# Second layer of a two-layer cross attention: value products for batches 0 to 3, 4 to 6 and 7, with a fixed order on VectorE and earlier finishing

## The chip, the core and the metric

The kernel runs on one core of a Trainium2 chip. The metric is the device time of one execution in microseconds. The core has five engines that work side by side and meet at semaphores: PE (TensorE, matrix products; PEld is its loading of weights), DVE (VectorE, elementwise work and reductions), ACT (ScalarE), POOL (GpSimd) and SP (here only a queue that issues DMAs). Each engine takes its own instructions in the order in which they stand.

## The reference

Eight batches of 100 queries (`x`, 1024 wide) attend to a context of 1444 rows of 512. There are two layers, one after the other, both on the same context:

```python
# layer 0
Q = x @ Wq + bq;  K = ctx @ Wk + bk;  V = ctx @ Wv + bv
x = x + (softmax(Q @ K.T / 32, axis=keys) @ V) @ Wo + bo
# layer 1: the softmax runs over the queries, not over the keys
q = x @ Wq + bq;  k = ctx @ Wk + bk;  v = ctx @ Wv + bv
w = softmax(q @ k.T / 32, axis=queries)
y = w @ v + x
out = (y - mean(y)) * rsqrt(var(y) + 1e-6) * gamma + beta
```

All numbers are float32.

## The kernel before

The kernel folds the weights first: it multiplies Wq by Wk and, in layer 0, Wv by Wo, so that the context enters the scores and the weighted sums directly. Queries are held transposed in one tile, `xT` (128 partitions, 8 blocks of the feature dimension, 800 columns: 100 for each batch). Layer results are added into it.

The second layer goes through the batches one after the other in `alternated(b, ...)`. A batch has 48 steps n. At each step PE does one matmul of `A` (`weighted_rows`: softmax weights times context rows, four blocks of 100 columns, in a bank of the pool `psum2`) and one piece of the scores of batch b+2 (`scores`: 44 pieces of about 131 columns, in four banks of the pool `psum`, which has six). After the last step ACT copies A to a tile `A1T` (L524). When the scores of a batch are complete, ACT copies them to `prob` with a scale and a bias (L554), DVE turns `prob` into rows of keys with 16 block transposes (`transposed`, L589), and DVE and ACT make the softmax of it (`softmax_rows`: maxima L656, exponentials L658, reciprocals L661, products L662). POOL adds up the weights over the keys (`weight_sums`, ending at L680). At step 8 of every odd batch PE transposes two batches' sums into a bank of `psum` (`weight_totals`, tile `wsum_ps`, L687), and DVE reduces this bank to `r` (L689).

The values are applied afterwards, to A of several batches together. `seven_products` makes a product of two halves by two halves with seven products of halves instead of eight; its names are X, Z, Y, W, and X is used three times, Y twice. `put` and `add` take the banks' contents away: for the second layer both are additions into `xT` on DVE (`add_to_queries`, L612). The right-hand sums T (`right_sums`) are made of A by DVE; the left-hand sums of Wv by POOL in `project1_sums`. Before the change:

- batches 0 to 4 go through `project1_halves` (seven products, each 8 matmuls of 250 columns) after batch 5; the sums partly overwrite A in place;
- batches 5 and 6 go through `project1` (32 plain matmuls of 200 columns, L718) after batch 6;
- batch 7 goes through `project_last` at the end (L784).

In batch 5 the scores of batch 7 run at two pieces a step (`doubled`), so that they are complete after 22 steps.

`finish` brings a batch to its output: eight transposes on PE into two banks of `psum` (`untransposed`, tile `z`, L741), DVE adds the bias times r (L745) and takes statistics (L751, L756), DVE, POOL and ACT normalise (rstd L758 and L759, z L760, L762, L763), and POOL issues the output's DMA (L764). Before the change batches 0, 1 and 2 are finished during batch 6, from steps 0, 14 and 28 on; 3 and 4 around and inside `project1`; 5 and 6 during batch 7. Batch 7 ends the program: its output leaves in two halves, one by the SP queue and one by the ACT queue (L766 to L768).

PE's order is written out by hand (`tc.manual_schedule(engines={PE})`); that of the other engines comes from a scheduler. The pools give a bank to the next user in the order of the program, and the new user waits for the last reader of the old contents.

Of the kernel before, what the change touches and what calls it, by code (L numbers as in the profile page):

```python
# [24 lines left out]
F32 = mybir.dt.float32  # L25
# [5 lines left out]
P = 128  # L31
# [13 lines left out]
PT = 4  # L45
G = 4
GT = G * T
G1 = 5
SCALE = 1.0 / math.sqrt(E)
EPS = 1e-6  # L50

# [2 lines left out]
def two_layer_cross_attention(ctx: ExitStack, tc: tile.TileContext, a: dict, out: bass.AP):  # L54
# [18 lines left out]
        return stream.tile([P, E + L], F32, tag="unit", name=name)  # L73

    def wide(name):
        t = work.tile([P, LC * G1 * T], F32, tag="AT", name=name, bufs=2)
        return t[:, : LC * GT].rearrange("p (c t) -> p c t", c=LC)

    def row(name):
        return work.tile([P, E], F32, tag="row", name=name, bufs=3)  # L80

    def weight_rows(name):
        return work.tile([P, MC * T + QD * (-(-T // QD)) - T], F32, tag="wT", name=name, bufs=3)


    ones = const.tile([P, P], F32, tag="ones", name="ones")
# [36 lines left out]
    def run(*parts):  # L123

        parts = list(parts)
        while parts:
            parts = [g for g in parts if next(g, parts) is not parts]
# [19 lines left out]
                    skip_group_check=True,  # L147
                )

    def combine(to, x, y, op, engine=nc.vector):  # L150
        for t, p, q in zip(to, x, y):
            engine.tensor_tensor(t, p, q, op)

# [1 line left out]

        return [t[:, i, :] for i in range(n)]

    def left_sums(A, S, some=(0, 1, 2, 3), engine=nc.vector):
        A11, A12, A21, A22 = A
        todo = ((S[0], A21, A22, ALU.add), (S[1], S[0], A11, ALU.subtract))  # L160
        todo += ((S[2], A11, A21, ALU.subtract), (S[3], A12, S[1], ALU.subtract))
        for n in some:
            combine(*todo[n], engine)
# [7 lines left out]

    def seven_products(name, A, Bs, S, T_, nb, width, put, add, left=None, right=None):

        left, right = left or (lambda n: None), right or (lambda n: None)
        A11, A12, A21, A22 = A
        B11, B21, B12, B22 = Bs

        def pair(n, bank=bank):
            return [bank(f"{name}_{n}{j}") for j in range(2)]

        def product(banks, lhs, rhs, fresh):
            half_product(banks, lhs, rhs, fresh, nb, width)
# [12 lines left out]
        add(0, 0, Z)  # L198
        Y = pair("y")
        product(Y, S[0], T_[0], True)  # L200
        put(1, 1, Y)
        yield
        right(3)
        product(X, S[1], T_[1], False)
        put(0, 1, X)
        yield
        left(2)
        right(2)
        W = pair("w", bank2)
        product(W, A22, T_[3], True)  # L210
        yield
        left(3)
        product(X, S[2], T_[2], False)
        add(1, 1, X)
        put(1, 0, X)
        add(1, 0, W)
        yield
        product(Y, S[3], B22, False)
        add(0, 1, Y)
        yield  # L220


    def weight_products(name, left, right, l_width, r_width, scaled):
# [32 lines left out]

        A11, A12, A21, A22 = lefts(0, 0), lefts(1, 0), lefts(0, 1), lefts(1, 1)
        B11, B12, B21, B22 = rights(0, 0), rights(0, 1), rights(1, 0), rights(1, 1)
        extra = [work.tile([P, LC * G1 * T], F32, tag="AT", name=f"{name}_s{n}", bufs=2) for n in range(2)]
        S1 = [extra[i // 2][:, i % 2 * 768 : i % 2 * 768 + lh] for i in range(H)]  # L260
        T1 = [extra[i // 2][:, i % 2 * 768 + lh : (i % 2 + 1) * 768] for i in range(H)]

# [267 lines left out]
    def scores(s, layer, cT, softmax, alone=False):  # L530
# [29 lines left out]
            )  # L560
        w = s["rows"] = weight_rows(f"w{layer}_{b}")
        s["w"] = w[:, : MC * T].rearrange("p (c t) -> p c t", t=T)
        softmax(s, parts)
        yield

    def softmax0(s, parts):

        b, p = s["b"], s["p"]
        maxima = small.tile([T, len(parts)], F32, tag="maxima", name=f"maxima_{b}")
        for n, part in enumerate(parts):  # L570
            nc.vector.tensor_reduce(maxima[:, n : n + 1], p[:, part], AX.X, ALU.max)  # L571
# [7 lines left out]
        transposed(s, 0 if b else PT)  # L579

    def transposed(s, m0):

        p, w = prob[s["b"] % len(prob)], s["rows"]
        for q in range(-(-T // QD) - 1, -1, -1):
            for r in range(P // QD):
                nc.vector.transpose(  # L589
                    blocks(w, r, m0 * T + q * QD, T, MC - m0),  # L590
                    blocks(p, q, m0 * MR + r * QD, MR, MC - m0),
                )

    def blocks(t, quad, first, step, n):

# [12 lines left out]
    def add_to_queries(blocks, t0, width, banks):  # L608
        n = len(blocks) // len(banks)
        for j, ps in enumerate(banks):  # L610
            to = xT[:, blocks[j * n] : blocks[j * n] + n, t0 : t0 + width]
            nc.vector.tensor_tensor(to, to, ps[:, : n * width].rearrange("p (n t) -> p n t", n=n), ALU.add)  # L612

    def value_sums(w):

# [26 lines left out]

    def softmax1(s, parts):

        transposed(s, 0)
        for m in range(0, MC, GM):
            softmax_rows(s, m)
        weight_sums(s)
# [48 lines left out]
        left_sums(A, S, engine=nc.gpsimd)  # L697
        return A, S

    def project1_halves(A, S, At):  # L700

        n = G1 * T // 2
        Bs = [[At[:, 2 * k + i, g * n : (g + 1) * n] for i in range(2)] for g in range(2) for k in range(2)]
        t1 = work.tile([P, LC, GT], F32, tag="gT", name="o1_t1", bufs=3).rearrange("p c t -> p (c t)")
        T_ = ([t1[:, i * n : (i + 1) * n] for i in range(2)], Bs[0], Bs[2], Bs[1])

        def add(r, g, banks):
            add_to_queries([4 * r + i for i in range(4)], g * n, n, banks)

        run(seven_products("o1", A, Bs, S, T_, 4, n, add, add, right=lambda k: right_sums(Bs, T_, (k,))))  # L710

    def project1(b0, n, A, between):

        t0, t1 = b0 * T, (b0 + n) * T
        for e in range(EC):
            ps = bank(f"o1_{b0}_{e}")
            for k in range(LC):
                nc.tensor.matmul(  # L718
                    ps[:, : n * T], wv1[:, k, e * P : (e + 1) * P], A[:, k, : n * T], start=(k == 0), stop=(k == LC - 1)
                )  # L720
            to = xT[:, e, t0:t1]
            nc.vector.tensor_tensor(to, to, ps[:, : n * T], ALU.add)
            if e == EC // 2 - 1:
                between()

    def untransposed(s):

# [25 lines left out]
    def normalise(s):  # L753
# [7 lines left out]
        if b < B - 1:  # L761
# [1 line left out]
            nc.gpsimd.tensor_tensor(z, z, beta[:T], ALU.add)  # L763
            nc.gpsimd.dma_start(out=out[b], in_=z)  # L764
            return
        for half, queue in ((slice(0, E // 2), nc.sync), (slice(E // 2, E), nc.scalar)):  # L766
            nc.vector.scalar_tensor_tensor(z[:, half], z[:, half], rstd, beta[:T, half], ALU.mult, ALU.add)
            queue.dma_start(out=out[b][:, half], in_=z[:, half])  # L768

# [32 lines left out]

        return scores(batches[b], layer, *loaded(load_features(b)), softmax, alone=True)

    def alternated(b, layer, softmax, dst, doubled=False):

        nxt = b + 2 < B  # L810
        c, *cT = loaded(load_rows(b), *([load_features(b + 2)] if nxt else []))
# [1 line left out]
        ahead = scores(batches[b + 2], layer, *cT, softmax) if nxt else iter(())  # L813
        for _ in range(MC * LC):
            next(A)
            for _ in range(2 if doubled else 1):
                next(ahead, None)
            yield

    key_bias = [c0, None]  # L820
# [36 lines left out]
    run(first_scores(0, 1, softmax1))  # L857
    run(steps)
    run(first_scores(1, 1, softmax1))
    A1 = {}  # L860

    finished = {(B - 2, 0): 0, (B - 2, 14): 1, (B - 2, 28): 2, (B - 1, 6): G1, (B - 1, 22): G1 + 1}
    finishing = []
    for b in range(B):
        if b in (0, G1, B - 1):
            n = {0: G1, G1: 2, B - 1: 1}[b]
            t = work.tile([P, LC * G1 * T], F32, tag="AT", name=f"A1T_{b}", bufs=2)
            t = t[:, : LC * n * T].rearrange("p (c t) -> p c t", c=LC)
            for i in range(n):
                A1[b + i] = (t, t[:, :, i * T : (i + 1) * T])  # L870
        for n, _ in enumerate(alternated(b, 1, softmax1, A1[b][1], b + 3 == B)):
            if b % 2 and n == 8:
                weight_totals(batches[b - 1 : b + 1])
            if (b, n) in finished:
                finishing.append(finish(batches[finished[b, n]]))
            finishing = [f for f in finishing if next(f, finishing) is not finishing]
        if b == B - 1:
            run(untransposed(batches[b]))
        if b == 1:
            AS = project1_sums(wv1)  # L880
        if b == G1:
            project1_halves(*AS, A1[0][0])
        if b == B - 2:
            run(finish(batches[G1 - 2]))
            project1(G1, 2, A1[G1][0], lambda: run(finish(batches[G1 - 1])))
        if b == B - 1:
            project_last(batches[b], A1[b][0])


# [22 lines left out]
```

## Time and profile before

| what | us |
|---|---|
| median of three runs | 642.72 (641.82 to 643.38) |
| the profiled execution's own time | 642.46 |
| its span, first to last instruction | 640.7 |
| PE busy in the span | 631.4 |
| DVE busy in the span | 450.0 |
| second layer, batch 3 (48 steps, A and scores) | 503.6 to 523.5 |
| batch 5, with doubled scores | 542.9 to 563.0 |
| seven products for batches 0 to 4 | 563.0 to 586.6 |
| batch 6, with three finishes | 586.6 to 600.3 |
| products for batches 5 and 6, with one finish inside | 600.5 to 612.2 |
| batch 7, with two finishes | 612.2 to 624.6 |
| last products, and the end of the span | 625.5 to 640.7 |

The mean granted clock of PE is 0.996 of full speed. A group in the profile is named by its line, engine and operation, with the tiles it writes and reads. In a timeline each row has the start, the busy time, the engine, the line and the operation; brackets at the end give the idle time of the engine ahead of it and who ended it. PE's float32 matmuls leave two records each, transposes one.

### The profile page before, as it was taken

How to read it: one execution, taken by the hardware profiler on the slowest of the kernel's cores; microseconds unless marked ns; L12 is line 12 of the kernel's file. 1: busy time of each engine (PE TensorE's matmuls, PEld its weight loads, DVE VectorE, ACT ScalarE, POOL GpSimd, SP SyncE). 2: the span in 40 equal slices, each digit the busy share in tenths (PEclk: the TensorE clock that was granted, in tenths of full speed). 3: DMA queues.
4: the chain of work that ended last, by engine and by line, in shares of the span. 5: the costliest groups of instructions: out<-in, count | busy, mean ns of one | idle time of the engine just before them, and what ended most of it. 6: DMA issues, size and time to landing. Idle time of an engine off the chain costs nothing.

```text
span 640.7 us, 9823 instructions
## 1 busy us (share of the span) xinstructions
PE 631.4 (99%) x3920; PEld 518.4 (81%) x3920; DVE 450.0 (70%) x848; ACT 132.2 (21%) x337; POOL 101.7 (16%) x121
## 2 busy tenths in 40 slices
PE   9999999999999999999999999999999999999994
PEld 8886445568885999999998655556999999999992
DVE  5999959669723775566655798238777655896994
ACT  1010010100203333212330000123433244330221
POOL 5000000009200000000010000007211222112773
PEclk9999999999999999999999999999999999999998
DMA  8928018000089788988996203055889998940122
GB/s 292 383 101 316 0 56 333 0 1 0 2 288 367 263 310 295 329 311 311 310 315 237 97 1 131 1 176 202 284 298 315 313 307 317 303 172 1 52 78 77
DMA packets 47961, 127.28 MB, mean 199 GB/s; under 512 B 3944, under 2 KB 6504, under 8 KB 47916
## 3 DMA queue, kind: packets, MB, share of 16 engines
q1 hardware_dynamic: 45454, 119.63, 53.8%
q0 software_dynamic: 2064, 6.56, 3.2%
q8 instruction: 31, 0.51, 0.3%
q10 hardware_dynamic: 398, 0.47, 0.2%
q14 instruction: 14, 0.11, 0.1%
HBM read 123.36 MB, written 3.28 MB: 198 GB/s over the span
## 4 chain that ended last, share of the span: by engine, by line
PE 84%; issue 5%; POOL 5%; DVE 4%; ACT 2%; POOLq 0%; DVEq 0%; ACTq 0%
PE s L542 23%; PE A L513 20%; PE qk_x L141 7%; PE g_x L141 5%; PE qk_y L141 4%; PE g_y L141 3%; PE vo_x L141 3%; DVE w L589 3%; PE o_x L141 3%; POOL z L763 2%; PE qk_w L141 2%; PE vo_y L141 2%; PE qk_z L141 2%; PE g_w L141 2%; PE g_z L141 2%
## 5 line engine op out<-in xcount | busy, mean ns | idle before, releaser
L513 PE MATMUL A<-w,c 120*128 120x100 f32 (+1 forms) x1536 | 245.9, 265 | 0.0
L513 PEld LDWEIGHTS A<-w,c 120*128 120x128 f32 (+1 forms) x1536 | 215.5, 190 | 0.8
L589 DVE STREAM_TRANSPOSE w<-prob 32x384 f32<-32x384 f32 (+1 forms) x256 | 143.7, 561 | 46.4 <-ACT prob L554 15.8
L542 PE MATMUL s<-cT,g0T 128*100 128x131 f32 (+2 forms) x592 | 122.7, 296 | 0.0
L542 PE MATMUL s<-cT,g1T 128*100 128x131 f32 (+2 forms) x592 | 119.3, 296 | 0.0
L542 PEld LDWEIGHTS s<-cT,g0T 128*100 128x100 f32 x592 | 78.3, 167 | 8.3
L542 PEld LDWEIGHTS s<-cT,g1T 128*100 128x100 f32 x592 | 77.5, 167 | 8.9 <-ACT g1T L418 0.9
L554 ACT ACTIVATE prob<-s,c 100x393 f32<-100x393 f32 (+2 forms) x64 | 35.1, 560 | 116.9 <-PE s L542 116.6
L658 ACT ACTIVATE w<-w,negmax 120x100 f32<-120x100 f32 (+1 forms) x96 | 34.8, 364 | 75.1 <-DVE negmax L656 75.1
L469 POOL TENSOR_SCALAR xT<-xT,L_xattn_bo 128x800 f32<-128x800 f32 x8 | 20.8, 2607 | 133.1 <-PE qk_x L141 133.1
L571 DVE TENSOR_REDUCE maxima<-prob 100x1 f32<-100x394 f32 (+3 forms) x32 | 16.6, 528 | 28.1 <-ACT prob L554 27.9
L141 PE MATMUL qk_x<-qk 128*128 128x256 f32 x128 | 29.8, 393 | 0.0
L141 PEld LDWEIGHTS qk_x<-qk 128*128 128x128 f32 x128 | 24.7, 197 | 4.1 <-ACT qk L278 0.4
L850 POOL DMA_DIRECT2D vectors<-in_L_xattn_gamma x1 | 0.6, 602 | 163.2 <-DMA c<-in_ctx 163.2
L675 POOL TENSOR_TENSOR part<-w 120x500 f32<-120x500 f32 x8 | 10.0, 1248 | 103.5 <-PE s L542 47.3
L302 DVE SCALAR_TENSOR_TENSOR qk_L_xattn_bk<-qk,L_xattn_bk,qk_L_xattn_bk 128x1024 f32<-128x1024 f32 x14 | 17.9, 1276 | 4.0 <-DMA qk<-in_L_xattn_WqT 3.9
L612 DVE TENSOR_TENSOR xT<-xT,o_x 128x400 f32<-128x400 f32 (+1 forms) x24 | 13.5, 600 | 7.9 <-PE o_x L141 7.8
L418 ACT ACTIVATE g1T<-g_x,k 128x400 f32<-128x400 f32 x6 | 3.6, 594 | 74.2 <-PE g_x L141 63.8
L658 ACT ACTIVATION_READ_ACCUMULATOR w<-w,negmax 120x1 f32 (+1 forms) x96 | 17.9, 187 | 0.0
L763 POOL TENSOR_TENSOR z<-z,vectors 100x1024 f32<-100x1024 f32 x7 | 16.5, 2356 | 8.3 <-ACT z L762 8.3
L762 ACT ACTIVATE z<-z,rstd 100x1024 f32<-100x1024 f32 x7 | 8.0, 1149 | 39.7 <-POOL rstd L759 39.6
L662 DVE TENSOR_TENSOR w<-w,rtotal 120x400 f32<-120x400 f32 (+1 forms) x24 | 15.2, 633 | 0.5
(216 smaller groups left out, 871.8 us busy)
## 6 DMA issues: line engine op xcount, KB each, us to landing
cT<-in_ctxT SPq DMA_DIRECT2D x64, 722.0 KB, 6.7
c<-in_ctx SPq DMA_DIRECT2D x48, 768.0 KB, 7.5
c<-in_ctx SPq DMA_DIRECT2D x16, 512.0 KB, 6.6
vo<-in_L_xattn_Wo SPq DMA_DIRECT2D x8, 512.0 KB, 7.2
qk<-in_L_xattn_WqT SPq DMA_DIRECT2D x8, 512.0 KB
qk<-in_L_xattn_WqT SPq DMA_DIRECT2D x15, 256.0 KB, 5.4
qk<-in_L_xattn_WkT SPq DMA_DIRECT2D x15, 256.0 KB, 6.2
c<-in_ctx SPq DMA_DIRECT2D x16, 224.0 KB, 6.4
```

The costliest lines, as they stand in the source:

```text
L141: nc.tensor.matmul(banks[n // per][:, n % per * width : (n % per + 1) * width], lhs[i][:, n * P : (n + 1) * P], rhs[i], start=(fresh and i ...
L302: nc.vector.scalar_tensor_tensor(acc, src, cols[v][:, h : h + 1], acc, ALU.mult, ALU.add)
L469: nc.gpsimd.tensor_scalar(xT[:, e, :], xT[:, e, :], out_bias[:, e : e + 1], None, ALU.add)
L513: nc.tensor.matmul(ps[:, k * T : (k + 1) * T], c[m // CQ][:r, m % CQ, k * P : (k + 1) * P], w[:r, m, :], start=(m == 0 and k == 0), stop=( ...
L542: nc.tensor.matmul(banks[n // per][:T, cuts[n] - o : cuts[n + 1] - o], q[:, k, t0 : t0 + T], cT[k][:, cuts[n] : cuts[n + 1]], start=(k == ...
L554: nc.scalar.activation(p[:, part], ps[:T, : part.stop - part.start], AF.Identity, bias=key_bias[layer][:T, b : b + 1], scale=SCALE,)
L571: nc.vector.tensor_reduce(maxima[:, n : n + 1], p[:, part], AX.X, ALU.max)
L589: nc.vector.transpose(blocks(w, r, m0 * T + q * QD, T, MC - m0), blocks(p, q, m0 * MR + r * QD, MR, MC - m0),)
L612: nc.vector.tensor_tensor(to, to, ps[:, : n * width].rearrange("p (n t) -> p n t", n=n), ALU.add)
L658: nc.scalar.activation(w[:r, m0 + m, :], w[:r, m0 + m, :], AF.Exp, bias=negmax[:r, m : m + 1], accum_out=total[:r, m : m + 1])
L662: nc.vector.tensor_tensor(w[:r, grp, :], w[:r, grp, :], rtotal[:r].unsqueeze(2).to_broadcast([r, GM, T]), ALU.mult)
L763: nc.gpsimd.tensor_tensor(z, z, beta[:T], ALU.add)
```

## The change

It touches the second layer only.

- The value products are made in three sets: batches 0 to 3, batches 4 to 6, and batch 7. The first two go through a new `project1`, both with seven products: 8 matmuls of 200 columns each for the first, of 150 for the second. The first set runs right after batch 3, the second right after batch 6. The sums T have a tile of their own and are all made at the start.
- Within `project1` DVE's instructions are kept in program order (the wrapper `Vector`). In the first set the 16 block transposes of batch 5's softmax are dealt out between the additions: 3 each after Z, Y, the second X and W, and the rest at the end. For this `softmax` has become a generator (`s["softmax"]`), and `transposed` yields after each transpose.
- W's additions come right behind W where `put` is `add`.
- The doubled scores in batch 5 are gone: one piece a step everywhere.
- Finishes begin at other steps: batches 0, 1 and 2 in batch 4 (steps 2, 16, 30), batch 3 in batch 5 (step 4), batches 4, 5 and 6 in batch 7 (steps 2, 15, 28).
- The last output's first half leaves by the ACT queue, its second by SP.
- The AT tiles are 400 columns by 4 instead of 500 by 4.

```diff
-G1 = 5
+SETS = (range(0, 4), range(4, 7), range(7, 8))
...
+        if put is add:
+            add(1, 0, W)
         yield
         left(3)
         product(X, S[2], T_[2], False)
         add(1, 1, X)
         put(1, 0, X)
-        add(1, 0, W)
+        if put is not add:
+            add(1, 0, W)
...
-        softmax(s, parts)
+        s["softmax"] = softmax(s, parts)
+        if (layer, b) != (1, SETS[0][-1] + 2):
+            run(s["softmax"])
...
-                nc.vector.transpose(
+                vector.transpose(
                     blocks(w, r, m0 * T + q * QD, T, MC - m0),
                     blocks(p, q, m0 * MR + r * QD, MR, MC - m0),
                 )
+                yield
...
+    def project1(bs, A, S, At, between):
+
+        n, t0 = len(bs) * T // 2, bs[0] * T
         Bs = [[At[:, 2 * k + i, g * n : (g + 1) * n] for i in range(2)] for g in range(2) for k in range(2)]
...
+        sums = work.tile([P, LC, GT], F32, tag="gT", name=f"o1_{t0}_t", bufs=3).rearrange("p c t -> p (c t)")
+        T_ = [[sums[:, (2 * k + i) * n : (2 * k + i + 1) * n] for i in range(2)] for k in range(4)]
...
+        vector.in_order = True
+        right_sums(Bs, T_)
+
+        room = iter((0, 3, 3, 3, 3))
+        for _ in seven_products(f"o1_{t0}", A, Bs, S, T_, 4, n, add, add):
+            for _ in range(next(room, 0)):
+                next(between, None)
+        run(between)
+        vector.in_order = False
...
-        for half, queue in ((slice(0, E // 2), nc.sync), (slice(E // 2, E), nc.scalar)):
+        for half, queue in ((slice(0, E // 2), nc.scalar), (slice(E // 2, E), nc.sync)):
...
-            for _ in range(2 if doubled else 1):
-                next(ahead, None)
+            next(ahead, None)
...
-    finished = {(B - 2, 0): 0, (B - 2, 14): 1, (B - 2, 28): 2, (B - 1, 6): G1, (B - 1, 22): G1 + 1}
+    finished = {(4, 2): 0, (4, 16): 1, (4, 30): 2, (5, 4): 3, (7, 2): 4, (7, 15): 5, (7, 28): 6}
...
+    for bs in SETS:
+        t = wide(f"A1T_{bs[0]}").rearrange("p c t -> p (c t)")[:, : LC * len(bs) * T]
+        t = t.rearrange("p (c t) -> p c t", c=LC)
+        for i, b in enumerate(bs):
+            for n, _ in enumerate(alternated(b, 1, softmax1, t[:, :, i * T : (i + 1) * T])):
+                if b % 2 and n == 8:
+                    weight_totals(batches[b - 1 : b + 1])
+                if (b, n) in finished:
+                    finishing.append(finish(batches[finished[b, n]]))
+                finishing = [f for f in finishing if next(f, finishing) is not finishing]
+            if b == 1:
+                AS = project1_sums(wv1)
+        if b < B - 1:
+            project1(bs, *AS, t, batches[bs[-1] + 2]["softmax"] if bs[0] == 0 else iter(()))
+    run(untransposed(batches[B - 1]))
+    project_last(batches[B - 1], t)
```

More of the change, by code (lines that the diff above doesn't have):

```diff
@@ L75, in wide @@
     def wide(name):
-        t = work.tile([P, LC * G1 * T], F32, tag="AT", name=name, bufs=2)
-        return t[:, : LC * GT].rearrange("p (c t) -> p c t", c=LC)
+        return work.tile([P, LC, GT], F32, tag="AT", name=name, bufs=2)
     def row(name):
@@ L83, in weight_rows, with __getattr__, call @@
         return work.tile([P, MC * T + QD * (-(-T // QD)) - T], F32, tag="wT", name=name, bufs=3)
+    class Vector:
+        in_order = False
+        def __getattr__(self, op):
+            def call(*args):
+                ins = getattr(nc.vector, op)(*args)
+                return tc.keep_in_program_order(ins) if self.in_order else ins
+            return call
+    vector = Vector()
     ones = const.tile([P, P], F32, tag="ones", name="ones")
@@ L148, in half_product, with combine @@
                 )
-    def combine(to, x, y, op, engine=nc.vector):
+    def combine(to, x, y, op, engine=vector):
         for t, p, q in zip(to, x, y):
@@ L156, in chunks, with left_sums @@
         return [t[:, i, :] for i in range(n)]
-    def left_sums(A, S, some=(0, 1, 2, 3), engine=nc.vector):
+    def left_sums(A, S, some=(0, 1, 2, 3), engine=vector):
         A11, A12, A21, A22 = A
@@ L258, in weight_products @@
         B11, B12, B21, B22 = rights(0, 0), rights(0, 1), rights(1, 0), rights(1, 1)
-        extra = [work.tile([P, LC * G1 * T], F32, tag="AT", name=f"{name}_s{n}", bufs=2) for n in range(2)]
+        extra = [wide(f"{name}_s{n}").rearrange("p c t -> p (c t)") for n in range(2)]
         S1 = [extra[i // 2][:, i % 2 * 768 : i % 2 * 768 + lh] for i in range(H)]
@@ L578, in softmax0 @@
         nc.scalar.activation(p, p, AF.Copy, scale=rtotal)
-        transposed(s, 0 if b else PT)
+        yield from transposed(s, 0 if b else PT)
     def transposed(s, m0):
@@ L611, in add_to_queries @@
             to = xT[:, blocks[j * n] : blocks[j * n] + n, t0 : t0 + width]
-            nc.vector.tensor_tensor(to, to, ps[:, : n * width].rearrange("p (n t) -> p n t", n=n), ALU.add)
+            vector.tensor_tensor(to, to, ps[:, : n * width].rearrange("p (n t) -> p n t", n=n), ALU.add)
     def value_sums(w):
@@ L643, in softmax1 @@
     def softmax1(s, parts):
-        transposed(s, 0)
+        yield from transposed(s, 0)
         for m in range(0, MC, GM):
@@ L698, in project1_sums @@
         return A, S
-    def project1_halves(A, S, At):
-        n = G1 * T // 2
+    def project1(bs, A, S, At, between):
+        n, t0 = len(bs) * T // 2, bs[0] * T
         Bs = [[At[:, 2 * k + i, g * n : (g + 1) * n] for i in range(2)] for g in range(2) for k in range(2)]
-        t1 = work.tile([P, LC, GT], F32, tag="gT", name="o1_t1", bufs=3).rearrange("p c t -> p (c t)")
-        T_ = ([t1[:, i * n : (i + 1) * n] for i in range(2)], Bs[0], Bs[2], Bs[1])
+        sums = work.tile([P, LC, GT], F32, tag="gT", name=f"o1_{t0}_t", bufs=3).rearrange("p c t -> p (c t)")
+        T_ = [[sums[:, (2 * k + i) * n : (2 * k + i + 1) * n] for i in range(2)] for k in range(4)]
         def add(r, g, banks):
[L708 to L724, printed above, removed]
+            add_to_queries([4 * r + i for i in range(4)], t0 + g * n, n, banks)
+        vector.in_order = True
[6 more added lines that the diff above has]
+        vector.in_order = False
     def untransposed(s):
@@ L803, in first_scores, with alternated @@
         return scores(batches[b], layer, *loaded(load_features(b)), softmax, alone=True)
-    def alternated(b, layer, softmax, dst, doubled=False):
+    def alternated(b, layer, softmax, dst):
         nxt = b + 2 < B
@@ L859, in two_layer_cross_attention @@
     run(first_scores(1, 1, softmax1))
-    A1 = {}
-    finished = {(B - 2, 0): 0, (B - 2, 14): 1, (B - 2, 28): 2, (B - 1, 6): G1, (B - 1, 22): G1 + 1}
+    finished = {(4, 2): 0, (4, 16): 1, (4, 30): 2, (5, 4): 3, (7, 2): 4, (7, 15): 5, (7, 28): 6}
     finishing = []
[L864 to L887, printed above, removed]
+    for bs in SETS:
[14 more added lines that the diff above has]
+    project_last(batches[B - 1], t)
 def kernel(**inputs):
```

## The prediction

> **What bounds the kernel now.** I read the page first (its own span is 640.7 us; the profiled execution's time is 642.46 us, 0.26 below the median of 642.72, with 1.76 us outside the span), then busy time by stage of the second layer, then the timelines of PE, DVE, ACT and POOL there.
>
> ```profile
> span 640.7 us, 9823 instructions
> PE 631.4 (99%) x3920; PEld 518.4 (81%) x3920; DVE 450.0 (70%) x848; ACT 132.2 (21%) x337; POOL 101.7 (16%) x121
> ...
> 503.50:523.40 19.90, 19.90 (x189) 19.90 (x188) 13.16 (x27) 7.24 (x30) 3.62 (x7) 1.00 0.91 307
> 542.90:563.00 20.10, 20.10 (x187) 20.10 (x185) 17.45 (x37) 6.66 (x29) 3.60 (x7) 1.00 0.94 313
> 563.00:586.60 23.60, 23.60 (x114) 21.28 (x113) 19.17 (x38) 4.94 (x25) 3.81 (x7) 1.00 0.22 78
> ```
>
> In each line the first number is the stretch's length, then busy us of PE, weight load, DVE, ACT and POOL, clock, DMA share and GB/s. PE fills every stage of the second layer; the chain of waits, at 84% PE, says the same. So a microsecond of matmul removed or of PE waiting added is a microsecond of the end, and DVE counts only where PE waits for it.
>
> ```profile
> 503.08 9.46 DVE L589 STREAM_TRANSPOSE w<-prob 32x384 f32<-32x384 f32 x16 [4.18 <-POOL wsum L680]
> 507.02 0.38 PE L687 MATMUL wsum_ps<-ident,wsum 124*100 124x124 f32 x2
> 507.24 0.36 PE L513 MATMUL A<-w,c 120*128 120x100 f32 x2
> 512.57 0.42 DVE L689 TENSOR_REDUCE r<-wsum_ps 100x2 f32<-100x248 f32 x1
> ...
> 548.52 0.38 PE L687 MATMUL wsum_ps<-ident,wsum 124*100 124x124 f32 x2
> 552.04 0.42 DVE L689 TENSOR_REDUCE r<-wsum_ps 100x2 f32<-100x248 f32 x1
> ```
>
> This is what decides. At step 8 of each odd batch PE transposes the weight sums into a PSUM bank (wsum_ps) and DVE reduces that bank to r. In batch 3 DVE gets to r only 5.6 us after PE wrote the bank, because the sixteen transposes of the next weights stand ahead of it. Today nobody on PE waits for r; PE goes straight on at 507.24.
>
> ```profile
> 562.98 3.56 PE L141 MATMUL o_x<-A1T,wv 128*128 128x250 f32 x16
> 566.38 3.54 PE L141 MATMUL o_z<-A1T,wv 128*128 128x250 f32 x16
> 600.49 5.37 PEld L718 LDWEIGHTS o<-A1T,wv 128*128 128x128 f32 x32 [0.27 <-ACT A1T L524]
> 605.26 2.36 POOL L763 TENSOR_TENSOR z<-z,vectors 100x1024 f32<-100x1024 f32 x1 [1.26 <-ACT z L762]
> 605.36 3.35 DVE L760 SCALAR_TENSOR_TENSOR z<-z,mv,vectors 100x1024 f32<-100x1024 f32 x1
> 633.98 1.52 POOL L759 TENSOR_TENSOR rstd<-rstd,mhalf 100x1 f32<-100x1 f32 x1 [4.10 <-DVE rstd L758]
> 636.32 0.31 SPq L768 DMA_DIRECT2D out<-z  x1
> 636.99 0.57 ACTq L768 DMA_DIRECT2D out<-z  x1
> ```
>
> The first three give the price of value products (3.38 us from start to start for 8 matmuls of 250 columns, 1.69 ns a column; 5.37 us for 16 of 200, 1.68), the next two a DVE instruction held up by a POOL one, the last three the tail.
>
> [...] The kernel splits them into a pool of six (scores, products, z, wsum_ps) and one of two; six are what I count with. [...] the L760 operation of DVE took 3.35 us beside POOL's z, 1.27 us elsewhere.
>
> **Part by part.** Batches are b, steps n; a full batch of the second layer is 48 steps of one A and mostly one score matmul.
>
> 1. *Products.* Removed: 56 matmuls of 250 columns and 32 of 200 (20,400 columns). Added: 56 of 200 and 56 of 150 (19,600). 800 x 1.69 ns = **-1.35 us**. For 150 columns no row exists; 1.69 ns a column gives 0.25 us, above the 0.223 us that a 100-column A takes with the same 128 weight columns (96 records, two each, in 10.70 us of the chain), so weights should hide. If they didn't, 56 x 0.03 = 1.7 us at most.
> 2. *Start of a set.* Now PE waits 0.27 us (L718) for the ACT copy of A; afterwards X and Z read only the first half of the set, whose copies are older, so 5.4 us of products (set 0) or 4.0 (set 1) cover the copy: **-0.2 us**.
> 3. *Set 0, DVE in fixed order.* Eight sums of 200 columns at 0.28 us (250 columns stand 0.33 apart), sixteen adds of 400 at 0.52, sixteen transposes at 0.59: 20 us over 18.8 us of PE. What PE waits for is the X bank's second read before the third X product. PE enters that product 5 x 2.69 = 13.4 us after the set began; DVE by then has done the sums (2.7), put X (3.9), three transposes (5.7), Z (6.7), Y (8.8), three transposes (10.6), X again (11.6). 1.8 us spare: **0**; without cover, up to 1.5.
> 4. *Finishes 0 to 2 in batch 4.* The same 24 z transposes and DVE work as before in batch 6, now beside the rest of softmax 5: DVE 0.8 + 2.4 + 3.7 + 3 x 4.5 = 20.4 us in a phase of about 21.6 us. The three output DMAs (0.6 us of POOL each) come along, between batch 5's weight sums and later finishes; input loads are on SP and are not passed. Covered, but it can push batch 6's transposes late (next point).
> 5. *Finish 3 in batch 5 (step 4).* In the order of the changed program the six banks are full when PE reaches the first matmul of the fourth score bank (step 9): three score banks, both banks of z for batch 3, and wsum_ps. So that score matmul waits for r, and r stands on DVE behind all sixteen transposes of batch 6's weights. From batch 3's rows: phase start 503.6; PE is there at 507.24 plus one A (0.2) plus five z transposes (0.5), 4.3 us into the phase; r ends at 512.99, 9.4 us in. PE waits **5.1 us**, if DVE starts as promptly as in batch 3. It may not: finish 2's normalise stands ahead of the transposes, and ACT's z of finish 1 ahead of its copies of batch 6's scores to prob, which the transposes read. Finish 2's twin in batch 6 now ends 9.1 us after its first transpose (594.5 to 603.6); step 30 of batch 4 is at 556.3, giving 565.4 against a prompt start of 563.4: up to 1.9 later. I take 5.8, bounds 5.1 and 7.0. Queued behind this wait on PE is the rest of batch 5, whose scores feed softmax 7, so everything later shifts. In batch 5 now, scores run double and take their fourth bank before step 8; that cover goes.
> 6. *Set 1 against softmax 7.* Removing the doubled scores puts softmax 7 later. Transposes start 0.5 us before the end of batch 5 and take 9.46; from their end to the last normalised weight is 6.0 us (532.4 to 538.4); the sums of set 1 stand behind: T0 is ready 15.3 us after batch 6 starts. PE reaches Y after 10.7 (A alone) + 4.0 = 14.7. Wait about **+0.5**, bounds 0 and 1.2.
> 7. *Tail.* First half from ACT, last from SP: the last issue costs 0.31 instead of 0.57 us, **-0.26**. Three finishes now crowd into batch 7 instead of two. On POOL one costs 0.6 + 1.25 + 2.36 + 0.9 = 5.1 us, 15.3 for three, in some 20 us to the last rstd, and in DVE's order finish 6's rstd comes after z of batch 7. POOL was free 4.1 us before the last rstd; that slack goes: **+0.2**, bounds 0 and 1.2.
> 8. The narrower AT tiles and the wrapper around DVE issue no work: 0. W's adds now stand right behind W; that is in the order of point 3. SP's input loads keep their order and get slack during set 0.
>
> Sum: -1.35 - 0.2 + 5.8 + 0.5 - 0.26 + 0.2 = **+4.7 us** on 642.46, so 647.2 us; against the median it is +0.7%.
>
> **Rivals.** *No wait at r* (the other side): if r were placed or ran early enough, or a bank came free before step 9, points 1, 2, 6, 7 leave -1.1: 641.4. For it: in batch 5 now r comes 3.5 us after wsum_ps, not 5.6, and if PE arrived 5.1 us later in the phase the wait would be nothing. Against it: z of batch 3 only brings 0.5 us of that. Decides: r before or after 568.2 us. *DVE backlog*: the fixed order and finishes 0 to 2 collide with POOL's weight sums [...] (2.1 us a collision, 3.35 - 1.27), the transposes of batch 6 start 2 to 4 us late, and points 6 and 7 reach their upper ends: -1.55 + 8 + 1.2 - 0.26 + 1.2 = +8.6, 651.0. For: 20.4 of 21.6 us on DVE. Against: it has 4.1 us idle ahead of the transposes in every batch now. *Set 0 stalls as well*: the three transposes between adds let PE wait 1.5 us at the third X: 648.7. Against: 1.8 us spare.
>
> **How the numbers follow.** Forecast 647.2: 0.68; backlog 0.12; set 0 stall 0.10; no wait 0.10. Its own range from the bounds of 5 to 7: low -1.55 + 5.1 - 0.26 = +3.3 (645.8), high -1.55 + 7.0 + 1.2 - 0.26 + 1.2 = +7.6 (650.1). These ends need all bounds at once; with the small tail outside I take 645.2 to 649.6. What a measurement can tell here is about 0.2%, 1.3 us. Slower 0.90; the case without the wait, at 641.4 just on the bound, gives 0.05 faster and 0.05 the same.
>
> **What would show it.** Right: a PE wait of 5 to 7 us on s, released by DVE's r, around 568 to 574 us, once; value products with 2.69 us (200) and 2.02 us (150) each and no wait in set 0; a wait under 1.2 us at Y of set 1; POOL busy up to the last rstd. Wrong: no PE gap in batch 5, or PE gaps inside set 0, or 150-column matmuls at more than 0.26 us.

## The result, and the profile after

The changed kernel takes 652.44 us (median of four, 651.97 to 652.98) against 642.27 us: ratio 1.0156, 95% interval 1.0138 to 1.0174. It is 10.2 us slower; +4.7 was forecast. The profiled execution took 651.97 us with a span of 650.0. Its page, with PE's busy tenths and granted clock in 40 slices of 16.25 us:

```profile
span 650.0 us, 9942 instructions
PE 631.5 (97%) x3968; PEld 520.4 (80%) x3968; DVE 456.7 (70%) x864; ACT 132.2 (20%) x337; POOL 102.3 (16%) x121
PE   9999999999999999999999999999999999959894
PEclk9999999999999999999999999999999999979998
```

PE is busy for the same time as before, 631.5 against 631.4 us, in a span that is 9.3 us longer: PE stands still. That its busy time is equal is a coincidence. In wsum_late below, where PEclk is 9 in every slice but the last, PE is busy for 629.9 us, 1.5 us less than before; here slower matmuls take as much again. The slice at 569 to 585 us has both the idle time (a 5) and a lower clock (a 7). The timelines of POOL, DVE and PE there (start, busy us, engine, line, operation; idle time and releaser in brackets):

```profile
561.98 2.35 POOL L776 TENSOR_TENSOR z<-z,vectors 100x1024 f32<-100x1024 f32 x1 [1.26 <-ACT z L775]
562.25 3.16 DVE L773 SCALAR_TENSOR_TENSOR z<-z,mv,vectors 100x1024 f32<-100x1024 f32 x1
565.45 9.46 DVE L91 STREAM_TRANSPOSE w<-prob 32x384 f32<-32x384 f32 x16
567.88 0.38 PE L706 MATMUL wsum_ps<-ident,wsum 124*100 124x124 f32 x2
574.93 0.42 DVE L708 TENSOR_REDUCE r<-wsum_ps 100x2 f32<-100x248 f32 x1
575.40 0.76 PE L558 MATMUL s<-cT,g1T 128*100 128x131 f32 x2 [6.84 <-DVE r L708]
```

This is the forecast wait at its forecast place: the fourth score bank waits for r, and r stands behind sixteen transposes. It lies within the bounds of 5.1 to 7.0 us and 1.0 us over the value taken, 5.8, because the transposes start late: they follow finish 2's L773, which took 3.16 us beside POOL's z of finish 1, begun 0.27 us before it; six of the eight L773 in this trace took 1.27 or 1.28 us.

The windows of the same profile (length, then busy us of PE, PEld, DVE, ACT and POOL, clock, DMA share, GB/s) show what was not forecast:

```profile
570.00:572.00 2.00, 0.00 (x0) 0.00 (x0) 1.95 (x5) 0.00 (x0) 0.37 (x1) 1.00 0.85 302
572.00:574.00 2.00, 0.00 (x0) 0.00 (x0) 1.91 (x4) 0.00 (x0) 0.00 (x0) 0.53 0.19 74
574.00:576.00 2.00, 0.60 (x3) 0.59 (x4) 1.94 (x5) 0.08 (x1) 0.00 (x0) 0.50 0.00 0
576.00:578.00 2.00, 2.00 (x11) 1.99 (x10) 0.95 (x2) 2.00 (x11) 0.00 (x0) 0.50 0.02 4
578.00:580.00 2.00, 2.00 (x17) 1.99 (x16) 1.52 (x4) 1.06 (x7) 0.00 (x0) 0.76 0.47 171
```

While PE is idle its granted clock falls to one half, and it stays there for 3.6 us after PE has work again: 11 matmul records in 2 us at 0.50, against 21 or 22 at full clock. That is 0.6 x 0.50 + 2.0 x 0.50 + 2.0 x 0.24 = 1.8 us lost on top of the wait (the 0.6 is PE's busy time at clock 0.50 from 574 to 576). Set 1, on PE, DVE and POOL:

```profile
608.71 2.28 PE L154 MATMUL o_y<-o_t,wv_s 128*128 128x150 f32 x16 [0.65 <-DVE o_t L91]
612.33 2.31 PE L154 MATMUL o_x<-o_t,wv_s 128*128 128x150 f32 x16 [1.33 <-DVE xT L91]
608.71 1.67 DVE L91 TENSOR_TENSOR o_t<-A1T,o_t 128x150 f32<-128x150 f32 x2
610.30 0.94 DVE L91 TENSOR_TENSOR o_t<-A1T 128x150 f32<-128x150 f32 x2
608.50 1.42 POOL L694 TENSOR_TENSOR part<-w 120x500 f32<-120x500 f32 x1 [17.02 <-DVE w L681]
```

Y waits 0.65 us for T0, because softmax 7 is late; this is point 6. X waits another 1.33 us, because two pairs of sums took 1.67 and 0.94 us, and the first pair 0.53. The same softmax lets POOL start its weight sums of batch 7 (L694) just then. Set 0 has no wait inside. One product group of each set, and the tail:

```profile
525.10 2.87 PE L154 MATMUL o_z<-A1T,wv 128*128 128x200 f32 x16
605.86 2.20 PE L154 MATMUL o_z<-A1T,wv 128*128 128x150 f32 x16
643.82 0.69 POOL L772 TENSOR_TENSOR rstd<-rstd,mhalf 100x1 f32<-100x1 f32 x1
645.33 0.56 ACTq L781 DMA_DIRECT2D out<-z  x1
645.99 0.31 SPq L781 DMA_DIRECT2D out<-z  x1
```

Start to start, the groups of the two sets are 2.71 and 2.04 us apart where nothing waits. POOL's last rstd has no idle time ahead of it; before, it had 4.10 us.

### The profile page after: what moved, and what is told of

Its sections match the earlier page's. It is cut to its first block, busy times and chain, and to the rows that moved or that the text cites. A ratio compares the mean times of both kernels' runs of the same rounds, so it can differ in the third digit from the quotient of the medians.

```text
span 650.0 us, 9942 instructions
## 1 busy us (share of the span) xinstructions
PE 631.5 (97%) x3968; PEld 520.4 (80%) x3968; DVE 456.7 (70%) x864; ACT 132.2 (20%) x337; POOL 102.3 (16%) x121
## 5 line engine op out<-in xcount | busy, mean ns | idle before, releaser
L558 PE MATMUL s<-cT,g1T 128*100 128x131 f32 (+2 forms) x592 | 123.9, 299 | 6.8 <-DVE r L708 6.8
L558 PEld LDWEIGHTS s<-cT,g1T 128*100 128x100 f32 x592 | 79.0, 169 | 16.0 <-DVE r L708 7.0
L694 POOL TENSOR_TENSOR part<-w 120x500 f32<-120x500 f32 x8 | 12.1, 1507 | 116.2 <-DVE rstd L771 40.7
L91 DVE TENSOR_TENSOR xT<-xT,o_x 128x400 f32<-128x400 f32 (+1 forms) x32 | 16.0, 540 | 3.9 <-PE o_x L154 3.7
L754 PE MATMUL z<-ident,xT 128*100 128x128 f32 x64 | 16.8, 280 | 0.0
L775 ACT ACTIVATE z<-z,rstd 100x1024 f32<-100x1024 f32 x7 | 8.0, 1150 | 40.5 <-POOL rstd L772 40.5
```

Of the source, the lines that this page charges most:

```text
L91: ins = getattr(nc.vector, op)(*args)
L558: nc.tensor.matmul(banks[n // per][:T, cuts[n] - o : cuts[n + 1] - o], q[:, k, t0 : t0 + T], cT[k][:, cuts[n] : cuts[n + 1]], start=(k == ...
L694: add(part, w[:MR, 0:5, :], w[:MR, 5:10, :], ALU.add)
L754: nc.tensor.transpose(ps[:T, e * P : (e + 1) * P], xT[:, 4 * j + e, b * T : (b + 1) * T], ident)
```

## The experiments

All kernels run on one core beside the kernel before (642.27 to 642.45 us in these comparisons). Waits are PE's, in the second layer, over 0.3 us, in the profiled execution.

| run | median us | ratio (95%) | waits, us |
|---|---|---|---|
| changed kernel | 652.44 | 1.0156 (1.0138 to 1.0174) | 6.84 at r; 0.65, 1.33 in set 1 |
| wsum_late | 644.30 | 1.0032 (1.0019 to 1.0045) | 1.45, 1.34 in set 1 |
| finish3_late | 649.21 | 1.0104 (1.0089 to 1.0119) | 5.62 in set 1 |
| bank4_step14 | 650.68 | 1.0128 (1.0112 to 1.0143) | 4.4 at r; 0.6, 1.3 in set 1 |
| bank4_step18 | 648.02 | 1.0094 (1.0072 to 1.0115) | 2.7 at r; 0.9, 1.3 in set 1 |
| pool_sums_late | 642.80 | 1.0010 (1.0002 to 1.0018) | 1.43 in set 1 |
| doubled_again | 644.07 | 1.0025 (1.0015 to 1.0034) | 0.31, 1.34 in set 1 |
| finish3_in_6 | 646.16 | 1.0060 (1.0044 to 1.0076) | 3.42 in set 1 |
| finish3_in_6_pool | 642.97 | 1.0012 (1.0004 to 1.0020) | 1.73 in set 1 |
| pool_all_late | 641.32 | 0.9981 (0.9973 to 0.9990) | none |

### Is it the six banks? (wsum_late, finish3_late)

```diff
-                if b % 2 and n == 8:
+                if b % 2 and n == (30 if b == 5 else 8):
```

> The changed kernel with one edit: in batch 5 the weight sums of batches 4 and 5 are transposed and reduced at step 30 and not at step 8; finish 3 stays at step 4. Collision theory (fourth score bank, both z banks and wsum_ps together fill the six banks): the wait of 6.8 to 7.0 us for r goes, and with it the slow clock after it (about 1.6 us), so 652.4 - 8.6 = 643.8 us, within 1 us; set 1 keeps its waits of about 2 us. Rival (DVE sets the pace from set 0 to set 1, and the wait at r is only where PE's slack gathers): the wait comes back in front of the products of set 1, 5 us or more there, time 650 or more.

644.30 us: 8.1 us of the 10.2 go with this one number, and no wait for r is left. This and the next run show the collision in the banks. The clock stays full in this part of the program, too (PEclk 9 in every slice but the last). The rival's wait of 5 us in front of set 1 did not come.

```diff
-    finished = {... (5, 4): 3, ...}
+    finished = {... (5, 24): 3, ...}
```

> The changed kernel with one edit: finish 3 starts at step 24 of batch 5 and not at step 4; the weight sums stay at step 8. Collision theory: wsum_ps and four score banks are five, so no wait for r and no slow clock, -8.6 us; but finish 3's normalise now stands on DVE ahead of the transposes for softmax 7, which makes set 1 wait 1 to 2 us longer: 644 to 646 us. Rival (the cost is finish 3 in batch 5 at all): 650 or more, with as much PE idle as before in batches 5 and 6. Second rival (DVE pace): as in wsum_late, 5 us or more of wait in front of set 1.

649.21 us, above the range of the collision theory. The wait for r went, but a new one of 5.62 us came in front of Y. The timelines of ACT, DVE and PE show its chain:

```profile
581.57 0.59 ACT L570 ACTIVATE prob<-s,c 100x394 f32<-100x394 f32 x1 [0.68 <-PE s L558]
587.16 1.15 ACT L775 ACTIVATE z<-z,rstd 100x1024 f32<-100x1024 f32 x1 [5.00 <-POOL rstd L772]
588.21 0.94 ACT L570 ACTIVATE prob<-s,c 100x394 f32<-100x394 f32 x2
589.19 9.45 DVE L91 STREAM_TRANSPOSE w<-prob 32x384 f32<-32x384 f32 x16 [4.25 <-ACT prob L570]
604.97 4.34 PE L154 MATMUL o_y<-o_t,wv_s 128*128 128x150 f32 x16 [5.62 <-DVE o_t L91]
```

Finish 3's z (L775) stands on ACT between the copies of batch 7's scores to prob. It waits 5.00 us for POOL's rstd, which itself comes after batch 6's weight sums; the last two copies, the transposes and softmax 7 are late with it. I had expected finish 3 to be in the way on DVE; it was on ACT. The second rival, DVE's pace, forecast just such a wait, but DVE stood idle for 4.25 us ahead of these transposes. The 4.34 us of o_y, against 2.28, is again the lowered clock, as the windows show:

```profile
602.00:604.00 2.00, 0.00 (x0) 0.00 (x0) 0.97 (x4) 2.00 (x11) 0.00 (x0) 0.86 0.00 0
604.00:606.00 2.00, 1.03 (x4) 1.06 (x5) 1.98 (x4) 0.15 (x1) 1.24 (x1) 0.50 0.00 0
610.00:612.00 2.00, 2.00 (x17) 2.00 (x16) 0.97 (x4) 0.00 (x0) 0.00 (x0) 0.94 0.00 0
```

Against wsum_late: 5.62 - 2.79 more waiting and some 2.5 for slow matmuls (o_y 2.06, the next group 2.77 against 2.31) make 5.3, and 4.9 is measured.

### From what length on does a wait lower the clock? (bank4_step18, bank4_step14)

The order of the score pieces of batch 7 is changed so that the fourth bank is first touched at step 18 or 14; everything else is as in the changed kernel.

```diff
+        order = [(k, n) for k in range(LC) for n in range(n_pieces)]
+        if (layer, b) == (1, B - 1):
+            first = [(k, n) for k, n in order if n < 9][:18]
+            order = first + [kn for kn in order if kn not in first]
-        for k in range(LC):
-            for n in range(n_pieces):
+        for k, n in order:
```

> The changed kernel, but the scores of batch 7 touch their fourth bank first at step 18 and not at step 9; same matmuls, same sums, finish 3 and the weight sums where they were. Nine steps later, PE should wait for r only 2 to 3 us instead of 7. If the clock falls only after an idle time of some length between that and 7 us, PEclk stays 1.00 after the wait, and the time is 652.4 - 4.5 - 1.6 = 646.3 us. If the slow stretch grows in proportion with the wait, 0.5 us or so of it stays and PEclk shows it: 646.9 us. If clock and wait have nothing to do with each other, the 1.6 us stay: 647.9 us.

> As bank4_step18, with the fourth bank touched first at step 14: a wait of about 4 to 4.5 us. [...] the clock falls as after the wait of 7 us (about 1.6 us lost): 652.4 - 2.6 = 649.8 us. In proportion: 649.2 us. If the clock needs more idle time than this, 648.2 us.

The waits came out at 2.7 and 4.4 us, the medians at 648.02 and 650.68 us. Both lie above all three forecasts; at 4.4 us the first, in which the clock falls, is the nearest, 0.9 us below. Windows of bank4_step14:

```profile
574.00:576.00 2.00, 0.00 (x0) 0.00 (x0) 1.91 (x5) 0.00 (x0) 0.00 (x0) 0.57 0.91 361
576.00:578.00 2.00, 1.93 (x9) 1.94 (x10) 2.00 (x5) 1.42 (x8) 0.00 (x0) 0.50 0.18 56
578.00:580.00 2.00, 2.00 (x12) 2.00 (x11) 2.00 (x7) 2.00 (x13) 0.00 (x0) 0.50 0.56 52
580.00:582.00 2.00, 2.00 (x16) 2.00 (x16) 1.98 (x7) 1.03 (x6) 0.00 (x0) 0.72 0.86 329
```

And of bank4_step18:

```profile
574.00:576.00 2.00, 0.62 (x5) 0.62 (x6) 1.94 (x5) 0.10 (x1) 0.00 (x0) 1.00 0.66 265
576.00:578.00 2.00, 2.00 (x21) 2.00 (x20) 2.00 (x5) 2.00 (x12) 0.00 (x0) 1.00 0.60 36
```

After 4.4 us the clock is at one half for longer once PE works again than after 6.84 us: 1.93 x 0.50 + 2.0 x 0.50 + 2.0 x 0.28 = 2.5 us lost. The mean clocks of the windows in which it falls and recovers give an estimate of how long the whole stretch at one half is; the windows ahead of it and behind it are at 1.00, those inside at 0.50. In the changed kernel it falls at 572.12 us (0.53 from 572 to 574) and is full again at 578.96 (0.76 from 578 to 580); in bank4_step14 the same working gives 574.28 and 581.12, in finish3_late 603.44 and 610.24.

| kernel | wait | clock falls, into the wait | half clock for | PE works in it for | lost |
|---|---|---|---|---|---|
| changed kernel | 6.84 | 3.6 | 6.8 | 3.6 | 1.8 |
| finish3_late | 5.62 | 4.1 | 6.8 | 5.3 | 2.6 |
| bank4_step14 | 4.37 | 2.6 | 6.8 | 5.1 | 2.5 |

All figures are us. The stretch has the same length each time, and what is lost is half of the part of it in which PE works. So a longer wait need not lose more: more of the stretch passes while PE stands still anyway. Only these three traces have such a stretch ahead of PE's last matmul; in other executions it may have another length: two of bank4_step14 have a mean clock of 0.994 and 0.995, the profiled one 0.990.

After 2.7 us the clock stays at 1.00 in the profiled execution. But of four executions two took 646.49 and 646.93 us with a mean granted clock of 0.996, and two took 649.12 and 649.33 us with 0.992 and 0.994; the median lies between them and means little. The shorter two are near the first forecast, 646.3. The times at which the clock falls allow for such a split. It fell 2.6 us into the wait of bank4_step14. At the end of the program, where PE has nothing left to do, the mean clock of the last 8.48 us of the changed kernel is 0.63, and of the last 8.17 us of the kernel before 0.66, with 0.50 in the last windows of both: it fell 2.2 and 2.6 us after the last matmul. The seven other profiled executions without such a stretch have a mean clock of 0.995 to 0.997, which gives some 2 to 5 us, an estimate that takes the clock as full up to there. That it fell in the two longer executions of bank4_step18 is argued from their mean clock; no trace shows it.

What decides when the clock falls was not shown: it fell 2.6, 3.6 and 4.1 us into the three waits, and PE worked for 5.1, 3.6 and 5.3 us before it was full again.

### What makes set 1 wait? (pool_sums_late, doubled_again)

Both start from wsum_late. In pool_sums_late POOL's weight sums of batch 7 move from the softmax to behind the sums of set 1, and are given a first instruction that reads DVE's last sum:

```diff
+        if after is not None:
+            nc.gpsimd.tensor_copy(part[:, 0, 0:1], after[:MR, 0:1])
...
         right_sums(Bs, T_)
+        if bs[-1] == B - 2:
+            weight_sums(batches[B - 1], T_[3][1])
```

> wsum_late with one edit: POOL's weight sums of batch 7 (about 4.6 us) start only when DVE's last sum of set 1 is done (a one-column copy on POOL reads that sum and holds them back). [...] (DVE's four two-tile sums of set 1 took 1.68 and 0.94 us beside POOL and would take about 0.53 without): the eight sums take about 2 us and not 3.7, the wait at Y falls from 1.45 to 0.5 to 0.9 us and the one at X from 1.34 to 0.3 or less; 644.3 - 1.5 to 2 = 642.3 to 642.8 us. Rival (the waits of set 1 come only from softmax 7 being late): the sums keep their length, and the time stays at 644.3 us.

642.80 us, 1.5 less. DVE's sums in this run:

```profile
600.24 0.53 DVE L91 TENSOR_TENSOR o_t<-A1T 128x150 f32<-128x150 f32 x2
600.69 0.60 DVE L91 TENSOR_TENSOR o_t<-A1T,o_t 128x150 f32<-128x150 f32 x2
601.22 0.53 DVE L91 TENSOR_TENSOR o_t<-A1T 128x150 f32<-128x150 f32 x2
601.67 0.53 DVE L91 TENSOR_TENSOR o_t<-A1T,o_t 128x150 f32<-128x150 f32 x2
```

The wait at X (1.34) is gone with the overlap: DVE's sums were held up by POOL's operations (the second and third pairs took 1.68 and 0.94 us in wsum_late, 0.60 and 0.53 here), as L773 was beside POOL's z ahead of the wait for r. My figure for Y was wrong: it stayed at 1.43. Y needs T0 only, the first pair, which POOL had never slowed (0.53 us in wsum_late, too); its wait is softmax 7 alone.

doubled_again has the scores of batch 7 at two pieces a step in batch 5 again:

```diff
-            next(ahead, None)
+            for _ in range(2 if doubled else 1):
+                next(ahead, None)
```

> wsum_late with one edit: the scores of batch 7 run two for each A in batch 5 again, as in the kernel before; finish 3 stays at step 4 of batch 5. If the removed doubling is what makes set 1 wait, softmax 7 is done some us sooner and both waits of set 1 (2.8 us together) go: 641.5 us. Rival: with finish 3 in batch 5, the last two copies of scores to prob still stand on ACT behind finish 3's z, which waits for POOL's rstd; softmax 7 then gains 1 us at most, and the time is 643.3 us or more.

644.07 us: the rival's outcome. The copies on ACT:

```profile
580.77 1.04 ACT L570 ACTIVATE prob<-s,c 100x393 f32<-100x393 f32 x2
582.12 1.15 ACT L775 ACTIVATE z<-z,rstd 100x1024 f32<-100x1024 f32 x1 [0.31 <-POOL rstd L772]
583.18 0.94 ACT L570 ACTIVATE prob<-s,c 100x394 f32<-100x394 f32 x2
```

Scores that are complete some 4 us sooner start the transposes only 1.5 us sooner (584.15 against 585.65 us). Two things on ACT hold the copies: the exponentials of softmax 6 end at 580.86 us, so that the first copy comes over a microsecond after the last score matmul, and finish 3's z divides the copies. Y's wait falls to 0.31, X's stays. The doubling alone is worth 0.2 us between the medians (644.30 and 644.07), 1.1 us in the wait at Y.

### Is anything left besides these waits? (finish3_in_6, finish3_in_6_pool, pool_all_late)

finish3_in_6 is the changed kernel with the doubled scores, and with finish 3 in batch 6; finish3_in_6_pool adds the held-back weight sums of pool_sums_late.

```diff
-    finished = {... (5, 4): 3, ...}
+    finished = {... (6, 2): 3, ...}
```

> The changed kernel with finish 3 moved out of batch 5 to step 2 of batch 6, and the doubled scores in batch 5 as before; the weight sums at step 8 as in the changed kernel. Collision theory: no wait for r (the fourth score bank is taken at step 5), and ACT's copies of scores have nothing ahead of them, so softmax 7 starts several us sooner; set 1 waits 0 to 1.5 us, since POOL's weight sums can still fall on DVE's sums. 641.3 to 643 us. Rival (the half products themselves or the fixed DVE order cost something that has not been seen yet): 644 us or more with no PE wait that accounts for it.

> finish3_in_6 with POOL's weight sums of batch 7 held back as in pool_sums_late. If both theories hold, no PE wait over 0.4 us is left between batch 3 and the end, and what is left of the change is its products (-1.05 us) and the start of a set (-0.2): 641.0 to 641.5 us, faster than the kernel before by about 0.15 to 0.2%. Rival (gains of a microsecond in set 1 are given back in the tail, where POOL has three finishes to do): 642.4 us or more, the last rstd of POOL later against the last matmul by 1 us.

646.16 and 642.97 us, both over what the theories gave. Each number is one that the rival forecast, but its sign is missing: finish3_in_6 has a PE wait that accounts for the time, and in finish3_in_6_pool POOL's last rstd starts 2.3 us after the last matmul, as in finish3_in_6. Softmax 7 is early now (Y doesn't wait), but a third POOL instruction found the gap, in finish3_in_6_pool's timelines:

```profile
599.81 2.68 DVE L91 TENSOR_TENSOR o_t<-A1T 128x150 f32<-128x150 f32 x2
599.90 2.41 POOL L781 TENSOR_TENSOR z<-z,vectors 100x1024 f32<-100x1024 f32 x1 [0.41 <-ACT z L780]
603.37 2.31 PE L154 MATMUL o_x<-o_t,wv_s 128*128 128x150 f32 x16 [1.73 <-DVE xT L91]
```

POOL's z of finish 3 falls on the third pair of sums. In finish3_in_6 it comes on top of the weight sums: 3.42 us at X, and in three of its six executions (646.38 to 648.17 us) the mean clock is 0.994 or 0.992, so part of its loss is probably the clock again; in the profiled one (0.996) it is 1.00 from 598 to 614 us, through this wait. pool_all_late therefore puts this z behind the sums too, and keeps both in program order on POOL:

```diff
             weight_sums(batches[B - 1], T_[3][1])
+            shifted(batches[3])
...
+    def shifted(s):
+        b, z = s["b"], s["z"]
+        ins = nc.gpsimd.tensor_tensor(z, z, beta[:T], ALU.add)
+        if b == 3:
+            tc.keep_in_program_order(ins)
+        nc.gpsimd.dma_start(out=out[b], in_=z)
```

> finish3_in_6_pool with POOL's z of finish 3 (2.41 us, which fell on the third sum of set 1) also placed behind DVE's last sum, after the weight sums of batch 7; the same work in all. [...] the eight sums take 2.1 us and not 4.1, the last wait of 1.73 us at the third product group of set 1 goes, no PE wait over 0.4 us is left from batch 3 to the end, and the time is 642.97 - 1.7 = 641.2 us, 0.15% under the kernel before. Rival (the microseconds come back in the tail, since POOL now has batch 7's weight sums and z of finish 3 to do before the last three finishes): the wait goes, but the time stays at 642.5 us or more, and POOL's last rstd starts over 1 us later after the last matmul than in finish3_in_6_pool.

641.32 us, as the first forecast had it, 0.2% faster than the kernel before (ratio 0.9981, 0.9973 to 0.9990). What the products are worth can be read between two kernels without waits, this one and the kernel before. The first row is of the kernel before, the others are of pool_all_late:

```profile
522.14 1.25 PE L513 MATMUL A<-w,c 124*128 124x100 f32 x10
522.17 1.03 PE L529 MATMUL A<-w,c 124*128 124x100 f32 x8
523.04 2.90 PE L154 MATMUL o_x<-A1T,wv 128*128 128x200 f32 x16
```

Eight records of A end batch 3 in both; set 0 starts 0.87 us after the first of them (523.04 - 522.17). In the kernel before, the last two of the ten records are already the first A of batch 4, which so starts at 522.14 + 0.87 = 523.01. From there to PE's last matmul it takes 109.52 us (to 632.53), and from set 0 in pool_all_late 108.24 (523.04 to 631.28). So the half products and the start of a set do save, 1.3 us, and the rest of the 10.2 us was nearly all waiting and its consequences.

## Why the prediction was wrong

The direction and the main mechanism were right: the wait at r, once, at the fourth score bank, in the forecast stretch. The sum was too small, by 4.8 us for the profiled execution and by 5.5 us between the medians. The largest missing term is the clock after the wait, which the sum did not have; the others are point 6 and the value taken for the wait itself.

| point | forecast | measured |
|---|---|---|
| 1 and 2, products and start of a set | -1.55 | -1.3 (pool_all_late) |
| 3, set 0 in fixed order | 0 | 0, no wait |
| 5, wait at r | +5.8 (5.1 to 7.0) | +6.84, and +1.8 slow clock |
| 6, set 1 | +0.5 (0 to 1.2) | +0.65 at Y, +1.33 at X |
| 7, tail | -0.06 | +0.3 |

These measured terms give 9.6 us for the 9.5 us by which the profiled execution grew. That is a closer match than it should be: PE reached set 0 here at 522.37 us and batch 4 in the kernel before at 523.01. That is scatter ahead of the change, since wsum_late, the same kernel up to there, reached set 0 at 523.07. About half a microsecond is thus without a term.

Why the wait came out longer can be read from the starts of two batches. The prediction put the start of batch 3 at 503.6 us; as with batch 4 above, its first A stands at the end of a row of ten (the first row is of the kernel before, the second of the changed one):

```profile
502.30 1.25 PE L513 MATMUL A<-w,c 124*128 124x100 f32 x10
562.71 1.25 PE L529 MATMUL A<-w,c 124*128 124x100 f32 x10
```

So batch 3 started at 503.17 and batch 5 of the changed kernel at 563.58 us. The wait of 5.1 us that was read from batch 3 is the difference of two times from one start, so this error does not reach it. The transposes started 0.1 us ahead of batch 3 (503.08) and 1.9 us after the start of batch 5 (565.45), and PE arrived 4.8 and 5.0 us into the batch: 5.05 + 1.96 - 0.21 = 6.80, and 6.84 is measured.

- **Point 5 is the step that failed.** It took the wait for the whole price. The sum had no term for the clock, though a wait of 5 to 7 us was its main result: 1.8 us are lost after it. The wait itself was mis-sized within its bounds. The late case that point 5 names, 565.4 us, is what happened; only 0.7 of its 1.9 us had been counted. By the trace, 1.9 us of the lateness is L773 beside POOL's z (3.16 against 1.27 us); no experiment takes this overlap away.
- **The rival with a backlog on DVE** comes nearest with its number, 651.0, but partly by luck. A collision of DVE with POOL did make the transposes late, by 1.9 us against its 2 to 4, through POOL's z and not through the weight sums that it named. Against it stood an idle time of 4.1 us ahead of the transposes "in every batch"; ahead of batch 7's, in the kernel before, it was 1.07. It too had nothing for the clock.
- **Point 6** counted the wait for softmax 7 well (0.5 against 0.65), but took the sums at their free duration; with X it came to 1.98 us, over the bound of 1.2. That DVE takes longer beside POOL was read off L760 (3.35 us; the other seven in that trace took 1.27 to 2.04, not all 1.27) and priced for the transposes in a rival, but not for the sums of set 1, although the softmax that releases them releases POOL's weight sums. pool_sums_late shows this wait (1.34 us in wsum_late) to come from there.
- **Points 1 and 2** held: products run 2.71 and 2.04 us apart (forecast 2.69 and 2.02). At 150 columns that is 1.70 ns a column (2.04 us for 8 x 150), as at 250 (1.69): no time for weights shows. Seven of each take 33.3 us, against 34.4 us by the prices of 3.38 and 5.37 us that the prediction read before.
- **Point 4** held for PE: no wait in batch 4. It named the right danger, that batch 6's transposes are pushed late.
- **Point 7**: POOL is indeed busy up to the last rstd, which starts at 643.82 us without idle time. That costs nothing: it ends 2.97 us after PE's last matmul, as before (635.50 - 632.53), where the same rstd had taken 1.52 us beside DVE. SP's issue does end 0.27 us sooner after PE's last matmul (4.76 against 5.03), but from there to the end of the span it takes 3.65 us and not 3.13, and 3.5 to 3.8 us in wsum_late, finish3_in_6_pool and pool_all_late. Why the output's last half takes longer that way is open.
- The stall inside set 0 did not come. The rival without a wait is what wsum_late comes near, and it still is 0.3% slower than before, through set 1.

## What to carry to other kernels

Count the banks that are held at each step, and ask which engine frees the last one and what stands ahead of it there: two transposes on PE moved by 22 steps were worth 8 us here. A forecast that contains a PE wait of some microseconds must price the clock after it: 1.8 to 2.6 us in the three traces with waits of 4.4 to 6.8 us, and by the mean clock perhaps at times from 2.7 us on. And when one event releases both DVE and POOL, expect them to meet: hold the one that nobody waits for (1.5 us here, 644.30 against 642.80).

## What the runs showed of the hardware

- In these runs the clock loss did not grow with the wait: 1.8 us after 6.84, 2.6 us after 5.6, 2.5 us after 4.4, none in the traces with 3.4 (finish3_in_6) and 2.7 (bank4_step18); executions of bank4_step18 are 2.5 us apart (646.7 against 649.2 us, means of two each). In the three traces with a loss the clock fell 2.6 to 4.1 us into the wait and stayed at one half for 6.8 us, of which the wait hid a part.
- Two DVE sums of 150 columns took 0.53 us without POOL at work (pool_sums_late, 601.22 us), 1.67 us beside POOL's weight sums (changed kernel) and 2.68 us beside its z (finish3_in_6_pool). POOL's own instructions took 1.42 us against 1.26 and 2.41 against 2.36; where DVE's L773 had begun first (changed kernel, 582.66 us, 1.27 us long), POOL's first weight sum took 2.20 us.
